# Two transformer layers in one kernel: weights of the second layer loaded into the first ffn's tiles, and a new order at the end of the second attention

## The chip, the cores and the metric

The kernel runs on one core of a Trainium2 chip. The metric is device time in microseconds (us) of one execution, the median of several runs. The engines are named as in the profile: PE is TensorE (PEld its weight loads), DVE is VectorE, ACT is ScalarE, POOL is GpSimd, and SP is SyncE, which here only issues DMAs. A name such as L921 is line 921 of the kernel before the change, unless the text says otherwise.

## The reference

The input is x of shape (4, 1024, 512): 4 sequences of 1024 tokens, 512 features, all in float32. Two layers follow each other, and each has the same outer form:

```
xn = layernorm(x)
x  = x + attention(xn) * silu(ffn(xn))
```

Layer 0's attention is linear attention with 16 heads of 32 features and an exponential decay per head, computed in chunks with a running state, between a qkv projection and an output projection. Its ffn is two linear layers with ternary weights, 512 to 2048 to 512, each behind a normalisation of its input, with gelu between them.

Layer 1's attention is softmax attention without a mask, 16 heads of 32 features. The first half of each head's q and k is rotated by position:

```
q, k, v = heads(x @ wq.T), heads(x @ wk.T), heads(x @ wv.T)
q, k    = rope on the first 16 of the 32 features of each head
y       = softmax(q @ k.T / sqrt(32)) @ v
return merge(y) @ wo.T
```

Layer 1's ffn has integer weights, from which 128 is subtracted, with a scale for each output feature:

```
lin(x, wq, scale) = x @ ((float(wq) - 128) * scale[:, None]).T
ffn(x) = lin(silu(lin(x, wq_gate, s_gate)) * lin(x, wq_up, s_up), wq_down, s_down)   # 512 -> 1408 -> 512
```

## The kernel before

The 4096 tokens are 32 tiles of 128 tokens (`NTILE`), in 8 blocks of 512 (`NBLK`, 4 tiles each, `TPB`). The kernel has four stages, one after the other: attention 0 (to about 628 us), the first ffn (to 1164), attention 1 (to 2668), and the second ffn (to the end). In the stages of interest the order of PE's instructions is the order in which the program writes them. The order on DVE, ACT, POOL and SP is made by a scheduler, except for operations that are marked with `tc.keep_in_program_order`, which keep their place among each other. Tiles come from pools with a fixed number of buffers, so that a new tile waits until its buffer's last reader is done.

**First ffn.** A loop over g takes one chunk c of 128 hidden features of one block per step (16 chunks, `NH0`). `hidden` (L563) makes the products `fc`, gelu on ACT, and the two halves hp (L583 on DVE) that carry a float32 value as two rounded parts; `proj` (L618) accumulates `pj`, some steps behind. `prep_in` (L541) loads a tile x0f of the next block and makes xq on DVE (L550) every third step. `gate` (L628) ends a tile: y (L640, DVE), tanh (ACT), two DVE products, the sum with x on POOL, the store of x1 on SP, and the moments of the new row for the next layernorm. `norm1` (L649) turns four rows' moments into scale and shift, with a root made of small DVE operations (`root`, L107). `wfc` are four tiles of 8 KB a partition.

**Start of attention 1.** Its pools open when those of the first ffn close. The weights wk, wq and wv are loaded by POOL DMAs (L752 to L758) into tiles of their own, wo later by SP. `heads_in` (L805) is a list of chains of products for one group of four heads: projections (L779), and the copies and the partial rotation of q and k, for which parts of raw tiles (tag `raw`, two buffers) are moved between partitions by DMAs (L830), with DVE L833 and POOL L835. `late` (L785) is the layernorm on ACT of the last four tiles, which the first ffn had not turned yet.

**Main loop of attention 1.** There are 32 units (sequence, group of four heads, half of the queries), and 8 steps a unit (`TB`), so 256 steps s; a second position e = s − 10 (`LAG`) runs behind. In step s PE does, in this order: two pairs of score products `sq` (`top`, L921), whose row maxima DVE reduces (`mx`, L925); the product y of e − 1 with v (`weigh`, L967); then the scores `sk` again, transposed, for e (`expo`: L948, and L954 which subtracts the maxima mT); and ACT makes the exponentials pT of e in two halves (L959, three buffers). At the end of a unit `turn_max` (L927) turns the maxima into mT (L937, DVE). POOL sums the eight pT of a unit into part (L1068, L1070); `total` (L858) and `divide` (L866) turn that sum into the divisor (zs, four reciprocals L874 on DVE) and yT (L875, POOL). For the last unit the sum is not made on POOL: PE totals each pT by itself (`z_last`). From s = 256 the loop has no `sq` any more, only the trailing y and sk. Products sq and sk share three buffers of two PSUM banks (`ring`). Between the pieces, `advance` lets PE do parts of chains that are queued: projections of the next group, or `wo_out` (L878), which makes four tiles of s and stores them (so, L892 and L893).

After the loop eight chains of `wo` remain, four of unit 30's half and four of the last.

**Second ffn.** `prep2` (L1090) loads xs and makes the two parts xp of a block (ACT copy L1097, DVE difference L1098). `weight` (L1105) loads a chunk of integer weights into `wint` (four buffers, L1111) and subtracts 128 on DVE (L1113); 33 chunks in the order of use. `gated` (L1134) makes gate and up (L1140), `down` (L1157) accumulates dn, `gate` (L1167) ends a tile: z, tanh (L1176), two products on DVE, the sum on POOL (L1179), the store (L1180). `most` (L1201) is the largest magnitude of each weight chunk; if one is above 4095, a second version of the whole ffn runs behind a branch, which these inputs never take.

Of the kernel before, what the change touches and what calls it, by code (L numbers as in the profile page):

```python
# [19 lines left out]
P = 128  # L20
# [15 lines left out]
def kernel(ctx, tc, ins, out):  # L36
# [44 lines left out]

    layer0 = ctx.enter_context(ExitStack())
# [42 lines left out]

    def transpose_to(dst, src, name, on_scalar):

        t = tr(f"tr_{name}")
        for k in range(4):
            nc.tensor.transpose(t[:, k, :], src[:, k * P : (k + 1) * P], ident)  # L130
        if on_scalar:
            nc.scalar.copy(dst, t)  # L132
        else:
            nc.vector.tensor_copy(dst, t)
# [8 lines left out]
    wfc = [f0w.tile([P, FF0], F32R, tag=f"wfc{k}", name=f"wfc{k}") for k in range(KD)]  # L143
# [383 lines left out]
    with ExitStack() as es:  # L527
# [8 lines left out]
        hparts, sums, mvs, x1s, xnTp = {}, {}, {}, {}, {}  # L536
# [4 lines left out]
        def prep_in(blk, i):  # L541
# [5 lines left out]
            x = p2.tile([P, D], F32, tag="x", name=f"x0f_{t}")  # L547
            nc.sync.dma_start(out=x, in_=x_t[t])
# [100 lines left out]
        def norm1(blk):  # L649

            ts = slice(blk * TPB, (blk + 1) * TPB)
            root(st1[:, ts, 1], 1e-5, p2, f"n{blk}", True)
            nc.vector.scalar_tensor_tensor(
                shift[:, ts], st1[:, ts, 0], -1.0, st1[:, ts, 1], ALU.mult, ALU.mult
            )

# [21 lines left out]
        pending = None  # L678
        for g in range(NH0 * NBLK + 2 + 2 * TPB):
            blk, c = divmod(g, NH0)  # L680
            if blk < NBLK:
                if c >= 2 and c % 3 == 2 and c < 2 + 3 * TPB and blk + 1 < NBLK:
                    pending = prep_in(blk + 1, (c - 2) // 3)
                hidden(blk, c)
                if blk == 0 and wpj0 + c < NH0:
                    ternary("pj", wpj0 + c, raw0("pj", wpj0 + c, "f"))
# [15 lines left out]
            if blk and (c == 12 or (blk == NBLK and c == 9)):  # L702
                norm1(blk - 1)
# [17 lines left out]
    s1_t = s1.rearrange("(t p) d -> t p d", p=P)  # L721
    with ExitStack() as es:
# [3 lines left out]

        w0 = es.enter_context(tc.tile_pool(name="a1w", bufs=1, reuse_waits="tile"))
# [12 lines left out]
        W, xnTs, heads = {}, {}, {}  # L740
# [11 lines left out]
        for n in ("wk", "wq", "wv", "wo"):  # L752
            W[n] = w0.tile([P, KD, D], F32, tag=n, name=n)
        for n in ("wk", "xnT", "wq", "wv"):
            if n == "xnT":
                load1(0)
                continue
            nc.gpsimd.dma_start(out=W[n], in_=ins[n + "T"].rearrange("(k p) n -> p k n", p=P))  # L758
        cs = w0.tile([P, 2, N], F32, tag="cs", name="cs")
# [25 lines left out]
        def late(i):  # L785
# [5 lines left out]
            nc.scalar.activation(  # L791
                xn, x, AF.Identity, bias=shift[:, t : t + 1], scale=st1[:, t, 1:2]
# [178 lines left out]

        es.enter_context(tc.manual_schedule(engines={mybir.EngineType.PE}))
# [4 lines left out]
        for c in heads_in(0, 0, spread):  # L977
            chain = c
            advance(8)
        must, spare = deque(), deque()  # L980
        mx, mTs, pTs, ys, parts, lates, soon = {}, {}, {}, {}, {}, {}, {}
        for s in range(TB * nu + LAG + 1):
# [25 lines left out]
            if s == 2 * TB:  # L1008
                tc.keep_in_program_order(
# [6 lines left out]
            if s < TB * nu:  # L1016
# [5 lines left out]
                if j == TB - 1:  # L1022
# [3 lines left out]
                    del mx[u]  # L1026
            if 1 <= e <= TB * nu:
# [4 lines left out]
                if u == nu - 1:  # L1032
# [3 lines left out]
                    total(z_last, pTs[e - 1], kb, TB)  # L1036
                pTs.pop(e - 2, None)
                if kb == TB - 1:
# [3 lines left out]
                    if u == nu - 1:  # L1042
                        divide(units[u], yr, z_last)
            held = 0
            if s % TB == 0 and 0 < s <= TB * nu:
                turn_max(s // TB - 1)
            elif s % TB == 4 and 0 <= s // TB - 2 < nu - 1:
                u = s // TB - 2
                z = ring(f"z_{u}")[:, 0, :] if s >= TB * nu else acc1(f"z_{u}")
                total(z, parts.pop(u), 0, 1)  # L1050
                divide(units[u], ys.pop(u), z)
                b, g, qh = units[u]
# [7 lines left out]
            if 0 <= e < TB * nu:  # L1060
                u, kb = divmod(e, TB)
                pT = pTs[e] = p2.tile([P, 4, 512], F32, tag="pT", name=f"pT_{e}", bufs=3)
                expo(u, kb, pT)
                if u == nu - 1:
                    pass
                elif kb == 1:
                    parts[u] = p2.tile([P, 4, 512], F32, tag="part", name=f"part_{u}")
                    nc.gpsimd.tensor_tensor(parts[u], pTs[e - 1], pT, ALU.add)  # L1068
                elif kb:
                    nc.gpsimd.tensor_tensor(parts[u], parts[u], pT, ALU.add)  # L1070
            advance(4 - held)
        for new in [*soon.values(), (*units[-1][::2], yTs[B - 1])]:
            spare.extend(wo_out(*new, spread))
        for chain in spare:
            advance(8)
# [5 lines left out]
    def ffn1_slots():  # L1081
# [8 lines left out]
        def prep2(blk):  # L1090

            b, h = divmod(blk, 2)
            xs = p2.tile([P, KD, BLK], F32, tag="xs", name=f"xs_{blk}", bufs=1)
            xp = [a.bitcast(F32R) for a in xpair(f"xp1_{blk}")]
            for k in range(KD):
                nc.sync.dma_start(out=xs[:, k, :], in_=xnT_d[b][k, :, h * BLK : (h + 1) * BLK])
                nc.scalar.copy(xp[0][:, k, :], xs[:, k, :])  # L1097
                nc.vector.tensor_tensor(  # L1098
                    xp[1][:, k, :], xs[:, k, :], xp[0][:, k, :].bitcast(F32), ALU.subtract
                )  # L1100
            return xp

        ws = {}

        def weight(n, c):  # L1105
            q = p2.tile([P, KD, P], I32, tag="wint", name=f"{n}_int{c}", bufs=4)
            if n == "down":
                src = ins["wq_downT"][c * P : (c + 1) * P, :].rearrange("p (k n) -> p k n", n=P)
            else:
                src = ins[f"wq_{n}T"][:, c * P : (c + 1) * P].rearrange("(k p) n -> p k n", p=P)  # L1110
            nc.sync.dma_start(out=q, in_=src)  # L1111
            w = ws[n, c] = wp.tile([P, KD, P], F32R, tag=f"{n}{c}", name=f"w{n}{c}")
            nc.vector.tensor_scalar(w, q, -128.0, None, ALU.add)  # L1113

        xp = prep2(0)
        sg = wp.tile([P, NH1], F32, tag="sg", name="sg")
        nc.sync.dma_start(out=sg, in_=ins["s_gate"])
        su = wp.tile([P, NH1], F32, tag="su", name="su")
        nc.sync.dma_start(out=su, in_=ins["s_up"])
        for c in range(NH1 + 2):  # L1120
            for n, d in (("gate", c), ("up", c), ("down", c - 2)):
                if 0 <= d < NH1:
                    weight(n, d)
        sdb = wp.tile([P, D], F32, tag="sdb", name="sdb")
        nc.sync.dma_start(out=sdb, in_=ins["s_down"].partition_broadcast(P))

        sg2 = wp.tile([P, NH1], F32, tag="sg2", name="sg2")
        nc.vector.tensor_scalar(sg2, sg, 0.5, None, ALU.mult)
        sgu = wp.tile([P, NH1], F32, tag="sgu", name="sgu")
        nc.vector.tensor_tensor(sgu, sg2, su, ALU.mult)  # L1130

# [190 lines left out]
    with ExitStack() as es1:  # L1322
        again = ffn1_slots()
# [77 lines left out]
```

## Time and profile before

| what | us |
|---|---|
| median of 3 runs | 3192.12 (3191.96 to 3195.52) |
| profiled execution | 3187.48 |
| its span in the profile | 3185.7 |
| PE busy in the span | 3103.5 |
| DVE busy | 1874.3 |
| POOL busy | 1512.6 |
| ACT busy | 1196.4 |
| last product of the first ffn ends | 1164.3 |
| last product of attention 1 ends | 2667.86 |
| first product of the second ffn starts | 2676.76 |
| last product of the second ffn ends | 3173.45 |

The times of instructions are those of the one profiled execution, counted from the start of its span. In a row of the waits, the columns are engine, line and operation that waited, what it waited for, the sum, the number of times and the longest. In a row of the timeline or of the chain, they are start, length, what ran, and in brackets the idle time before it and what ended that.

### The profile page before, as it was taken

To read this page: it belongs to the slowest core of one execution; us is meant where nothing else is said; L and a number is where in the kernel's file an instruction comes from. 1 tells how busy PE (TensorE), PEld (TensorE's weight loads), DVE (VectorE), ACT (ScalarE), POOL (GpSimd) and SP (SyncE) were. 2 spreads that over 40 slices of the span, in tenths; PEclk is the share of its full clock that TensorE was granted. 3 is DMA by queue.
4 is the path that set the end of the run, shared out by engine and by line. 5 is a ranking of instruction groups with operands and counts; after the bars stand their busy time and mean duration, and the time that the engine had idled before them with its cause. 6 is when DMAs were issued, how large, how long until landed. Compare 5 with 4: busy or idle time off the path is not lost.

```text
span 3185.7 us, 61092 instructions
## 1 busy us (share of the span) xinstructions
PE 3103.5 (97%) x26257; PEld 1763.6 (55%) x26257; DVE 1874.3 (59%) x2628; ACT 1196.4 (38%) x1695; POOL 1512.6 (47%) x618
## 2 busy tenths in 40 slices
PE   9999999999999989999999999999999988999998
PEld 5555555577777864344344444443344325888886
DVE  4444555478887866666555565655555634755554
ACT  2111111155655533444444444444444442333322
POOL 1000000034443445888988888988988850000001
PEclk9999999999999999999999999999999999999999
DMA  3111111212222331100001000100000005222112
GB/s 129 54 56 58 53 54 41 67 46 90 81 70 67 116 118 46 34 9 8 14 13 40 13 10 15 38 15 15 15 13 13 12 1 159 87 67 73 63 50 68
DMA packets 97655, 158.46 MB, mean 50 GB/s; under 512 B 13024, under 2 KB 26592, under 8 KB 97248
## 3 DMA queue, kind: packets, MB, share of 16 engines
q1 hardware_dynamic: 96560, 151.33, 15.2%
q8 instruction: 207, 3.39, 0.4%
q0 software_dynamic: 816, 3.15, 0.3%
q14 instruction: 72, 0.59, 0.1%
HBM read 104.10 MB, written 41.94 MB: 46 GB/s over the span
## 4 chain that ended last, share of the span: by engine, by line
PE 84%; DVE 10%; ACT 2%; issue 1%; DMA 1%; SPq 1%; POOL 1%; POOLq 0%; ACTq 0%; DVEq 0%
PE sk L948 9%; PE sq L921 8%; PE y L967 8%; PE qk L331 7%; PE dn L1162 5%; PE up L1140 5%; PE gate L1140 5%; PE v1ps L779 4%; PE wq L779 3%; PE v0ps L305 3%; PE wo L314 3%; PE wo L779 3%; PE pj L623 3%; PE wk L779 3%; PE fc L570 3%; PE sk L954 2%
## 5 line engine op out<-in xcount | busy, mean ns | idle before, releaser
L1070 POOL TENSOR_TENSOR part<-part,pT 128x2048 f32<-128x2048 f32 x186 | 854.4, 4594 | 19.3 <-ACT pT L959 10.0
L925 DVE TENSOR_REDUCE mx<-sq 128x2 f32<-128x1024 f32 x512 | 603.7, 1218 | 398.6 <-PE sq L921 397.5
L959 ACT ACTIVATE pT<-sk 128x1024 f32<-128x1024 f32 x512 | 496.4, 1022 | 625.5 <-PE sk L954 619.6
L948 PE MATMUL sk<-wqT,wkT 32*128 32x512 f32 x2048 | 325.8, 640 | 3.7 <-DVE mx L925 3.7
L921 PE MATMUL sq<-wkT,wqT 32*128 32x512 f32 x2048 | 320.3, 638 | 8.3 <-ACT pT L959 6.3
L967 PE MATMUL y<-pT,v 128*32 128x512 f32 x2048 | 283.5, 606 | 12.8 <-ACT pT L959 12.8
L1179 POOL TENSOR_TENSOR th<-th,x 128x512 f32<-128x512 f32 x32 | 41.4, 1293 | 493.6 <-DVE th L1178 393.0
L623 PE MATMUL pj<-wpj,hp 128*128 128x512 f32 x1024 | 265.8, 397 | 8.3 <-DVE hp L583 7.2
L591 POOL TENSOR_TENSOR sums<-sums,h 128x512 f32<-128x512 f32 x112 | 164.0, 1465 | 229.7 <-ACT h L575 220.9
L570 PE MATMUL fc<-xp,wfc 128*128 128x512 f32 x1024 | 261.5, 398 | 3.0 <-ACT h L575 2.1
L954 PE MATMUL sk<-mT,onesr 2*128 2x512 f32 x1024 | 236.2, 785 | 0.0
L338 POOL TENSOR_TENSOR qd<-qT,wqkv 128x512 f32<-128x512 f32 x32 | 43.1, 1346 | 404.7 <-ACT qT L336 379.2
L331 PE MATMUL qk<-xnT,wqkv 128*128 128x512 f32 x512 | 228.3, 599 | 0.7 <-ACT xnT L132 0.7
L623 PEld LDWEIGHTS pj<-wpj,hp 128*128 128x128 f32 x1024 | 190.1, 188 | 60.9 <-DVE hp L583 20.2
L570 PEld LDWEIGHTS fc<-xp,wfc 128*128 128x128 f32 x1024 | 187.9, 189 | 44.3 <-ACT h L575 5.0
L1140 PE MATMUL gate<-xp,wgate 128*128 128x512 f32 x704 | 180.1, 398 | 8.9 <-DVE wgate L1113 8.9
L1140 PE MATMUL up<-xp,wup 128*128 128x512 f32 x704 | 179.5, 396 | 1.0 <-DVE h L1147 1.0
L1162 PE MATMUL dn<-wdown,hp 128*128 128x512 f32 x704 | 177.8, 394 | 0.0
L1068 POOL TENSOR_TENSOR part<-pT,pT 128x2048 f32<-128x2048 f32 x31 | 141.1, 4553 | 71.2 <-ACT pT L959 71.2
L948 PEld LDWEIGHTS sk<-wqT,wkT 32*128 32x128 f32 x2048 | 97.4, 183 | 134.6 <-issue 113.8
L583 DVE TENSOR_TENSOR hp<-h,hp 128x512 fp32r<-128x512 f32 x128 | 119.1, 931 | 78.0 <-ACT hp L580 77.7
L967 PEld LDWEIGHTS y<-pT,v 128*32 128x32 f32 x2048 | 41.8, 108 | 214.4 <-issue 186.2
(216 smaller groups left out, 4566.9 us busy)
## 6 DMA issues: line engine op xcount, KB each, us to landing
s<-s SPq DMA_DIRECT2D x96, 256.0 KB
x<-x SPq DMA_DIRECT2D x36, 256.0 KB
x<-in_x SPq DMA_DIRECT2D x32, 256.0 KB
raw_fc<-in_w_fcT SPq DMA_DIRECT2D x32, 256.0 KB
x0f<-in_x SPq DMA_DIRECT2D x32, 256.0 KB
x0r<-in_x SPq DMA_DIRECT2D x32, 256.0 KB
x<-th SPq DMA_DIRECT2D x32, 256.0 KB
xnT<-xnT_d SPq DMA_DIRECT2D x8, 1024.0 KB
```

The costliest lines, as they stand in the source:

```text
L331: nc.tensor.matmul(a, lhsT=wqkv[k][:, c0 : c0 + P], rhs=xnTs[blk][:, k, :], start=(k == 0), stop=(k == KD - 1),)
L570: nc.tensor.matmul(a, lhsT=wfc[k][:, c * P : (c + 1) * P], rhs=xp[n][:, k, :].bitcast(F32R), start=(k == 0 and n == 0), stop=(k == KD - 1 ...
L623: nc.tensor.matmul(ds[i], lhsT=hparts[blk, c][n][:, i * P : (i + 1) * P], rhs=wpj[c], start=(c == 0 and n == 0), stop=(c == NH0 - 1 and n ...
L779: nc.tensor.matmul(out[r0 : r0 + HD, :], lhsT=lhsT[:, r0 : r0 + HD], rhs=rhs, start=start, stop=stop,)
L921: nc.tensor.matmul(sq[:, hh, :], lhsT=qT[r, q0 : q0 + P], rhs=kT[r, n * 512 : (n + 1) * 512], start=True, stop=True,)
L925: nc.vector.tensor_reduce(mx[:, qt, 2 * pair : 2 * pair + 2, n], sq, AX.X, ALU.max)
L948: nc.tensor.matmul(sks[h // 2][:, h % 2, :], lhsT=kT[r, kb * P : (kb + 1) * P], rhs=qT[r, qh * 512 : (qh + 1) * 512], start=True, stop=False,)
L959: nc.scalar.activation(pT[:, 2 * pair : 2 * pair + 2, :], sks[pair], AF.Exp, scale=QKS)
L967: nc.tensor.matmul(y[r, :], lhsT=v[:, kb, r], rhs=pT[:, h, :], start=(kb == 0), stop=(kb == TB - 1),)
L1070: nc.gpsimd.tensor_tensor(parts[u], parts[u], pT, ALU.add)
L1140: nc.tensor.matmul(a, lhsT=ws[n, c][:, k, :], rhs=xp[m][:, k, :], start=(k == 0 and m == 0), stop=(k == KD - 1 and m == 1),)
L1162: nc.tensor.matmul(ds[i], lhsT=hparts[blk, c][n][:, i * P : (i + 1) * P], rhs=w, start=(c == 0 and n == 0), stop=(c == NH1 - 1 and n == 1),)
```

## The change

Six parts, told in the order of the kernel.

1. A pool `w0` with four tiles of [128, 4, 512] float32 is opened before layer 0 and stays to the end. `wfc` of the first ffn uses these tiles; then wk, wq, wv and wo of attention 1; then the first 16 weight chunks of the second ffn, four to a tile. The POOL DMAs for wk, wq and wv are issued at the first step of the first ffn's closing phase, in a row.
2. In the first ffn the loads x0f are issued two steps before `prep_in` uses them.
3. `norm1` of the last block moves from the end of the first ffn into attention 1, behind the fourth chain of the first `heads_in`; the ACT operation of `late` keeps its program order.
4. The scales sg and su and their products become constants outside the second ffn.
5. End of attention 1: in each of the steps 244 to 255 one weight chunk of the second ffn is loaded into a raw tile and one converted (two in the last). From step 256 on, the scores sk and exponentials of e come before y of e − 1. The sums of pT move from POOL to DVE for those steps; the last unit's second four pT are summed there too, and its one total and its `divide` stand behind the second of the remaining `wo` chains. Unit 30's total comes two steps later. The parts xp of the second ffn's first block are made before the last four `wo` chains.
6. Second ffn: the other 21 weight chunks and the xs parts go through one tag `stage` of six buffers; s, x, z and th have four buffers; the very last tile is finished in two halves, with its sum on DVE; the `most` reductions keep their program order.

The core of the diff:

```diff
+    es1 = ExitStack()
+    w0 = es1.enter_context(tc.tile_pool(name="w0", bufs=1, reuse_waits="tile"))
+    shared = ("wk", "wq", "wv", "wo")
+    def shared_tile(tag, name):
+        return w0.tile([P, KD, D], F32, tag=tag, name=name)
...
-    wfc = [f0w.tile([P, FF0], F32R, tag=f"wfc{k}", name=f"wfc{k}") for k in range(KD)]
+    wfc = [
+        shared_tile(tag, f"wfc{k}").rearrange("p k n -> p (k n)").bitcast(F32R)
+        for k, tag in enumerate(shared)
+    ]
...
+        W = {}
         for g in range(NH0 * NBLK + 2 + 2 * TPB):
             blk, c = divmod(g, NH0)
+            if g == NH0 * NBLK:
+                for n in ("wk", "wq", "wv"):
+                    W[n] = shared_tile(n, n)
+                    tc.keep_in_program_order(
+                        nc.gpsimd.dma_start(
+                            out=W[n], in_=ins[n + "T"].rearrange("(k p) n -> p k n", p=P)
+                        )
+                    )
             if blk < NBLK:
...
+                if c % 3 == 0 and c < 3 * TPB and blk + 1 < NBLK:
+                    t = (blk + 1) * TPB + c // 3
+                    x0fs[t] = p2.tile([P, D], F32, tag="x", name=f"x0f_{t}")
+                    nc.sync.dma_start(out=x0fs[t], in_=x_t[t])
...
-            if blk and (c == 12 or (blk == NBLK and c == 9)):
-                norm1(blk - 1)
+            if blk and c == 12:
+                norm1(blk - 1, p2)
...
+    def weight(stage, pool, pinned=False):
+        m = len(ws)
+        n, c = needed[m]
+        q = stage(f"{n}_int{c}").bitcast(I32).rearrange("p (k n) -> p k n", n=P)
+        if n == "down":
+            src = ins["wq_downT"][c * P : (c + 1) * P, :].rearrange("p (k n) -> p k n", n=P)
+        else:
+            src = ins[f"wq_{n}T"][:, c * P : (c + 1) * P].rearrange("(k p) n -> p k n", p=P)
+        load = nc.sync.dma_start(out=q, in_=src)
+        j = m // 4
+        if j not in fours:
+            tag = quads[j] if j < len(quads) else f"wf{j}"
+            fours[j] = pool.tile([P, KD, D], F32, tag=tag, name=f"wf{j}")
+        w = ws[n, c] = fours[j][:, m % 4, :].bitcast(F32R).rearrange("p (k n) -> p k n", n=P)
+        if pinned:
+            tc.keep_in_program_order(load)
+        def less():
+            op = nc.vector.tensor_scalar(w, q, -128.0, None, ALU.add)
+            if pinned:
+                tc.keep_in_program_order(op)
+        return less
...
+    def parts1(blk, stage, pinned=False):
+        b, h = divmod(blk, 2)
+        xp = [a.bitcast(F32R) for a in xpair(f"xp1_{blk}")]
+        for k in range(KD):
+            xs = stage(f"xs_{blk}_{k}")
+            each = [
+                nc.sync.dma_start(out=xs, in_=xnT_d[b][k, :, h * BLK : (h + 1) * BLK]),
+                nc.scalar.copy(xp[0][:, k, :], xs),
+                nc.vector.tensor_tensor(
+                    xp[1][:, k, :], xs, xp[0][:, k, :].bitcast(F32), ALU.subtract
+                ),
+            ]
+            if pinned:
+                for op in each:
+                    tc.keep_in_program_order(op)
+        return xp
...
-        for c in heads_in(0, 0, spread):
+        for m, c in enumerate(heads_in(0, 0, spread)):
             chain = c
             advance(8)
+            if m == 3:
+                norm1(NBLK - 1, p2)
...
+        def exps(e):
+            if not 0 <= e < TB * nu:
+                return
+            u, kb = divmod(e, TB)
+            pT = pTs[e] = p2.tile([P, 4, 512], F32, tag="pT", name=f"pT_{e}", bufs=3)
+            expo(u, kb, pT)
+            k0 = TB // 2 if u == nu - 1 else 0
+            add = nc.vector if e + LAG >= TB * nu else nc.gpsimd
+            if kb == k0 + 1:
+                parts[u] = p2.tile([P, 4, 512], F32, tag="part", name=f"part_{u}")
+                add.tensor_tensor(parts[u], pTs[e - 1], pT, ALU.add)
+            elif kb > k0:
+                add.tensor_tensor(parts[u], parts[u], pT, ALU.add)
...
+            late_exp = s >= TB * nu
+            if late_exp:
+                exps(e)
...
+                    if kb < TB // 2:
+                        total(z_last, pTs[e - 1], kb, TB)
...
+            zu = (s - (6 if s >= TB * nu else 4)) // TB - 2
...
+            if TB * nu - 12 <= s < TB * nu:
+                nxt = weight(raw1, w0, True)
+                if loaded:
+                    loaded()
+                loaded = nxt
+                if s == TB * nu - 1:
+                    loaded()
+        soon = [*soon.values()]
+        for new in soon:
+            spare.extend(wo_out(*new, lambda name: ring(name)[:, 0, :]))
+        for m, chain in enumerate(spare):
+            advance(8)
+            if m == 1:
+                total(z_last, parts.pop(nu - 1), TB - 1, TB)
+                divide(units[-1], ys.pop(nu - 1), z_last)
+        xp1 = parts1(0, raw1, True)
+        for chain in wo_out(*units[-1][::2], yTs[B - 1], spread):
...
+        def stage(name):
+            return p2.tile([P, 512], F32, tag="stage", name=name, bufs=6)
+        xp = xp1
+        while len(ws) < len(needed):
+            weight(stage, w0 if len(ws) < 4 * len(quads) else wp)()
...
+            last = t == NTILE - 1
+            for h in range(2 if last else 1):
+                c = slice(h * D // 2, (h + 1) * D // 2) if last else slice(0, D)
+                nc.vector.tensor_tensor(z[:, c], d[:, c], sdb[:, c], ALU.mult)
+                nc.scalar.activation(th[:, c], z[:, c], AF.Tanh, scale=0.5)
+                nc.vector.scalar_tensor_tensor(th[:, c], th[:, c], 1.0, z[:, c], ALU.add, ALU.mult)
+                nc.vector.scalar_tensor_tensor(th[:, c], th[:, c], 0.5, s[:, c], ALU.mult, ALU.mult)
+                (nc.vector if last else nc.gpsimd).tensor_tensor(th[:, c], th[:, c], x[:, c], ALU.add)
+                nc.sync.dma_start(out=out_t[t][:, c], in_=th[:, c])
```

## The prediction

> **What bounds the kernel now.** I read the page's shares first. PE is busy for 97% of the span and holds most of the chain that ended last, so time can only come from the 3% in which PE stands, from PE running behind a slower clock, and from the ends of the span.
>
> ```profile
> PE 3103.5 (97%) x26257; PEld 1763.6 (55%) x26257; DVE 1874.3 (59%) x2628; ACT 1196.4 (38%) x1695; POOL 1512.6 (47%) x618
> PE 84%; DVE 10%; ACT 2%; issue 1%; DMA 1%; SPq 1%; POOL 1%; POOLq 0%; ACTq 0%; DVEq 0%
> ```
>
> A table of 80 us windows then finds that 3%. The columns behind the window are its length, busy time (instructions) of PE, PEld, DVE, ACT and POOL, the granted clock, the DMA share and GB/s.
>
> ```profile
> 1120.00:1200.00 80.00, 69.56 (x755) 52.22 (x753) 51.27 (x105) 30.24 (x50) 33.23 (x25) 0.98 0.34 110
> 2480.00:2560.00 80.00, 77.36 (x822) 29.71 (x816) 51.69 (x45) 33.82 (x40) 68.44 (x18) 0.98 0.03 10
> 2560.00:2640.00 80.00, 65.83 (x444) 18.24 (x440) 22.76 (x21) 34.49 (x38) 35.09 (x10) 1.00 0.00 1
> 2640.00:2720.00 80.00, 70.08 (x678) 50.28 (x671) 45.27 (x87) 20.86 (x35) 1.28 (x1) 0.94 0.61 191
> 2720.00:2800.00 80.00, 80.00 (x345) 64.42 (x344) 53.20 (x83) 25.75 (x41) 5.17 (x4) 1.00 0.19 60
> ```
>
> PE misses 10 to 14 us in each of three windows, and 2720 to 3120 has none to give: the second ffn runs at PE's own pace. The waits of PE name the holes, first from 2580 to 2720, then from 1160 to 1200:
>
> ```profile
> PE y L967 <- ACT pT L959: 12.8, 11, 1.2
> PE gate L1140 <- DVE wgate L1113: 8.9, 1, 8.9
> ```
> ```profile
> PE v1ps L779 <- DVE wqT L833: 3.1, 1, 3.1
> PE wq L779 <- DMA wq<-in_wqT: 2.5, 1, 2.5
> PE wq L779 <- DVE wkT L833: 1.7, 1, 1.7
> PE sq L921 <- POOL wqT L835: 1.5, 1, 1.5
> ```
>
> The 12.8 is not all that the tail loses. The chain in order of time shows the last steps as one file of links: scores, exponential, y, total, next scores.
>
> ```profile
> 2608.47 1.07 PE sk L948 x8
> 2609.86 1.03 ACT pT L959
> 2610.94 1.54 PE y L967 x6
> 2612.91 0.86 PE z_last L861 x6
> 2613.76 1.07 PE sk L948 x8
> ```
>
> From 2608.4 to 2634.9 a step takes 5.30, five times in a row. PE's work in it is sk 1.07, its max part 0.28, y 1.00 and total 0.86, which is 3.21; the rest is PE waiting for ACT.
>
> **The change, part by part** (us; minus is gained; against the profiled execution of 3187.48).
>
> *Start of the first ffn.* The waits of PE there are 0.9 for s L319 and 4.3 in four for hp L583. Issuing x0f two steps early takes its load out of the xq products' way and moves two of them, and one wpj, off DVE's queue ahead of hp_0_4; the longest wait is 2.65. DVE's products L550 take 0.50 alone and up to 1.52 when POOL is adding. I take two of 0.6 = −1.2; ends −2.5 (the whole 2.65) and 0 (another DVE step is late next).
>
> *First ffn to attention 1.* The three weight DMAs leave POOL ahead of the adds th_28 to th_31 (before, wq was issued at 1167.44, behind an add from 1165.78), so the 2.5 for wq goes, and norm1's chain (1176.56 to 1179.0) leaves DVE, so the 1.7 goes. But the path to the first sq does not run there. It is SP: x<-th L646 waits for POOL's th_31 (ends 1175.6), x_28's load is at 1176.11, and behind it 32 loads of raw_wk and raw_wq parts at 0.7 each end at 1198.67, feeding wqT at 1197.27 and sq at 1197.32. In the new DVE order the moments of row 29 stand before y_31 and wait for POOL, so y_31 ends about 1170.3 (1168.87 before), th_31 about 1176.55, and SP's file shifts by +1.0. I take +1.0: PE gets the same file of waits, redistributed. Ends: −1.5 (the waits of wq and wkT, 4.1, less what the file gives back) and +3.0 (norm1's 2.4 on DVE now ahead of late's first activation).
>
> *sg, su and their products at the kernel's start* cost nothing: two 0.4 issues on SP near 20 us, 0.33 on DVE near 30, between v products with PE's weights still loading; uncovered they would cost 0.7.
>
> *Steps 244 to 255, the twelve early conversions.* Each step gains a 256 KB load on SP (0.5; the window to 2560 moves 10 GB/s) and one conversion on DVE, 0.42 in its row:
>
> ```profile
> L1113 DVE TENSOR_SCALAR wgate<-gate_int x11: 416/423/429, 2676.2 to 2708.2; 128x512 fp32r<-128x512 int32 x11
> ```
>
> These ran with POOL idle; now POOL adds 128x2048 tiles, 4.53 each with 0.08 between. Behind each conversion on DVE are the two reductions mx (1.22 each) that free sq's banks. The nearest rows: neg_pj L189, a TENSOR_SCALAR from SBUF to SBUF, 0.48 alone, took 1.51 and ended 0.29 after POOL's instruction; mT L937 has 0.74 at least and 5.01 at most:
>
> ```profile
> 2589.47 3.72 DVE L937 SCALAR_TENSOR_TENSOR mT<-mh,second,mf 128x512 fp32r<-128x512 f32 x1 [5.74 <-ACT mh L935]
> 2574.32 27.86 POOL L1070 TENSOR_TENSOR part<-part,pT 128x2048 f32<-128x2048 f32 x6
> ```
>
> The fourth of those six adds ends at 2592.64, mT at 2593.19. The reductions L925 take 1.22 beside POOL too. So I let a conversion end 0.29 after the running add, and the next add start that much later. DVE's step is then 2.44 + 0.29 with the rest spent waiting, inside POOL's 4.9, and PE's step (2.26 + 1.00 + 1.35 = 4.61) keeps up by its spare banks. Followed step by step this makes the adds 1.1 late by the last one, and attention's end 1.4 later. Bounds: 0 (no blocking) and 12 × (4.53 + 0.29) = 57.8 (each conversion waits a whole add and PE with it).
>
> [...]
>
> *Tail of attention 1.* sk of step e now precedes y of e−1, so a step costs PE its own 3.21 and no wait for ACT (two exps, 1.94). The start is set on DVE: add 246 has moved there from POOL and stands before mT(31). It waits for POOL's add 245, 2592.64 + 1.1 = 2593.75, takes 2.28 (the 128x2048 add L467), and mT 0.55: 2596.6. Step 249's sk then starts at 2598.0 (2602.25 before). From there three steps of 3.21, one of 3.21 + 0.86 with unit 30's z, two of 2.35 without a total, then exp 255, which also waits for add 253 on DVE (exp 253 ends 2615, + 2.28 = 2617.3, no wait), and the last y's: wo starts at 2621.0 against 2639.65, −18.65. z_last's one late total stands among the wo chains, +0.86. Sum −17.8, conversions included; wo, 28.2, ends at 2649.8 against 2667.86. Cover that could fail: yT for the fifth chain is ready at 2621 + 0.86 + 7.0 (two chains) + 0.59 (zs) + 3.39 (four reciprocals) + 1.26 = 2634.1, needed 2636, 1.9 to spare. Ends −21.5 (no conversion blocks) and −8 (mT or an add late for every step).
>
> *Seam.* Before, the first gate product waited 8.90 for weights that SP issued at 2671.79, behind so's stores and four xs loads. Now twelve weights are there, and xp needs xs, whose loads sit on SP behind the stores so_3 and so_4 (2637 onward), land about 3.7 later as before (2668.99 to 2672.73), then copies and differences: ready about 2646, needed 2650. −8.9; the end on the other side is 0.
>
> *Cold start and weight rate behind it.*
>
> ```profile
> 2676.76 3.75 PE L1140 MATMUL gate<-xp,wgate 128*128 128x512 f32 x8 [8.90 <-DVE wgate L1113]
> 2716.54 1.86 PE gate L1140 x8
> ```
>
> Eight gate products took 3.75 after the idle stretch, 1.86 later, with the clock at 0.94 in this window. At that pace u3, behind seven groups (7 × 1.87 + 0.46), would have started at 2690.3; it started at 2693.5. −3.2. The 21 other weights come through six buffers; 33 took 40 before, 1.2 each, and weight 13 is needed 18.7 after the start: no stall. [...]
>
> *End.* The last tanh waits for a store, since th has two buffers:
>
> ```profile
> 3177.31 0.63 ACT L1176 ACTIVATE th<-z 128x512 f32<-128x512 f32 x1 [2.68 <-DMA out<-th]
> ```
>
> With four it starts near 3174.2; the row in two halves with its add on DVE, beside POOL's th_30, ends at 3178.75, where POOL ended at 3180.78. −2.0, ends −1.0 and −3.2. The max reductions `most` go from DVE's idle time at 2676 to 2739 into 33 later steps, 0.69 each, where DVE is two thirds busy: nothing.
>
> Sum: −1.2 + 1.0 − 17.8 − 8.9 − 3.2 − 2.0 = −32.1. 3187.48 − 32.1 = 3155.4 for a profiled execution. The median of the runs shown, 3192.12, lies 4.6 above the profiled one; I carry that on: 3160.0. All lower ends together give −40.3.
>
> **The rivals.** 0.2%, about 6.4 us, is what a measurement here can tell from no change.
>
> 1. *Conversions eat half of it.* Each waits half an add, 2.27 + 0.29 = 2.6, and half of that reaches PE through the banks that mx frees: 12 × 1.3 = 16, so −16, 3176. For: POOL is busy 68 of 80 in that window, and a banked reduction behind a blocked conversion frees nothing. Against: DVE is busy 52 of 80, PE has three bank pairs.
> 2. *The seam keeps its wait,* for xp instead of weights (SP's stores, or ACT's copies behind so, late): −8.9 and −3.2 fall away, −20, 3172. For: 4 us of margin worked out through four queues. Against: the loads are issued 13 us before they are needed.
> 3. *Slower.* One mechanism: in steps 244 to 255 a conversion waits for a whole add, the reductions behind it hold PE, and POOL's next add waits for the exponential that PE delays, so nothing overlaps. It decides from 32.1 / 12 = 2.7 a step; at the full 4.82 it is 57.8 − 32.1 + 1.4 (counted above) = +27, 3219.
> 4. *The change does not do what it says:* the last steps stay in file because ACT takes exp e only after PE's y has freed a pT buffer (three). Then the tail gives −4 (mT's earlier start), the sum −18, 3174. Against: pT of e−3 is free two steps before.
>
> **How the numbers follow.** Forecast case (−26 to −40) 0.60; rival 1 0.14, rival 2 and 4 0.12 together; nothing measurable, between rivals 1 and 3, 0.05; slower 0.09. Faster is 0.60 + 0.14 + 0.12 = 0.86. The forecast's own range is 3152 to 3166. Eight in ten must take in rivals 1, 2 and 4 with some more blocking: 3152 to 3184.
>
> **What would show it.** Right: wo starts near 2621 in the new trace, no wait of PE over 1 at the seam, its window at clock 1.00, steps 2.4 to 3.2 apart from 250, L1176's last wait gone, the first sq about 1 later than 1197.3 (counted from the end of the first ffn). Wrong: conversions of 3 to 5 with PE waiting for mx in steps 244 to 255; a first gate product waiting for L1098's successor; wo's fifth chain waiting for yT.

## The result

The changed kernel took 3148.71 us (median of 4 runs, 3146.93 to 3150.13) beside 3193.82 for the kernel before: a ratio of 0.9855, 95% interval 0.9838 to 0.9873. A second set of four later gave 3154.84 beside 3191.16, 0.9884 (0.9866 to 0.9902). So it is faster, by 36 to 45 us, where 32 was forecast; the first set lies below the forecast range. The profiled executions, 3187.48 and 3149.29, differ by 38.2. By stage of the two traces, with the prediction's terms beside:

| stage | before | after | change | predicted |
|---|---|---|---|---|
| start to first fc | 628.8 | 630.5 | +1.7 | 0 |
| first ffn, to its last pj | 535.6 | 533.7 | −1.9 | −1.2 |
| last pj to first sq | 32.95 | 33.99 | +1.0 | +1.0 |
| first sq to last wo | 1470.5 | 1459.7 | −10.8 | −17.8 |
| last wo to first gate | 8.90 | −0.07 | −9.0 | −8.9 |
| second ffn, first gate to last dn | 496.7 | 479.2 | −17.5 | −3.2 |
| last dn to the end | 12.25 | 10.53 | −1.7 | −2.0 |
| sum | | | −38.2 | −32.1 |

Five terms came as worked out or within 2 us. Two did not: the tail of attention gave 7 less, and the second ffn 14 more. The windows of the changed kernel, in the columns shown before:

```profile
2480.00:2560.00 80.00, 77.81 (x800) 29.59 (x792) 55.29 (x48) 32.00 (x39) 62.09 (x18) 0.91 0.10 29
2560.00:2640.00 80.00, 76.14 (x640) 27.80 (x634) 54.50 (x39) 38.63 (x44) 34.54 (x9) 0.96 0.09 27
2640.00:2720.00 80.00, 80.00 (x599) 62.53 (x593) 43.66 (x75) 27.78 (x45) 1.27 (x1) 1.00 0.55 178
2720.00:2800.00 80.00, 80.00 (x354) 66.24 (x354) 47.49 (x71) 24.32 (x39) 7.78 (x6) 1.00 0.23 73
```

PE waits for 4 us where it waited 14 (second row), and for nothing behind 2640. But the granted clock is 0.91 and 0.96 in the tail, where it was 0.98 and 1.00. And the last row holds 354 products where the kernel before had 345 in the same 80 us, PE busy throughout in both, the clock at 1.00 in both. The waits of PE from 2480 to the end show what is late next:

```profile
PE sk L1033 <- DVE mT L1016: 2.2, 1, 2.2
PE sk L1027 <- DVE mx L1004: 1.8, 3, 0.7
PE sq L1000 <- ACT pT L1038: 1.3, 4, 0.3
```

The waits for pT at y (12.8) and for the first weights (8.9) are gone; mT takes their place, for 2.2. From 1155 to 1220 the waits only changed hands:

```profile
PE v1ps L856 <- DVE wqT L912: 5.8, 1, 5.8
PE wk L856 <- DVE y L658: 2.3, 1, 2.3
...
PE sq L1000 <- POOL wqT L914: 0.4, 1, 0.4
```

Wk's second half now waits 2.3 for y_31 (1.0 before), since the moments of row 29 stand ahead of it on DVE, and v1ps 5.8 where it was 3.1; y_31 ended at 1169.99 and the last th sum at 1176.22, near the 1170.3 and 1176.55 forecast.

### The profile page after: what moved, and what is told of

The parts are those of the page before. It is cut to its first block, busy times and chain, and to the rows that moved or that the text cites. A ratio compares the mean times of both kernels' runs of the same rounds, so it can differ in the third digit from the quotient of the medians.

```text
span 3147.5 us, 61092 instructions
## 1 busy us (share of the span) xinstructions
PE 3088.4 (98%) x26233; PEld 1765.4 (56%) x26233; DVE 1905.1 (61%) x2638; ACT 1196.1 (38%) x1696; POOL 1501.4 (48%) x615
## 4 chain that ended last, share of the span: by engine, by line
PE 84%; DVE 11%; issue 2%; ACT 2%; POOL 1%; SPq 1%; DMA 0%; ACTq 0%; POOLq 0%; DVEq 0%
PE sk L1027 9%; PE sq L1000 8%; PE y L1046 8%; PE qk L350 7%; PE gate L1218 5%; PE up L1218 5%; PE dn L1240 5%; PE v1ps L856 4%; PE v0ps L324 3%; PE wo L333 3%; PE wo L856 3%; PE wq L856 3%; PE fc L588 3%; PE wk L856 3%; PE pj L641 3%; PE sk L1033 2%
## 5 line engine op out<-in xcount | busy, mean ns | idle before, releaser
L1067 POOL TENSOR_TENSOR part<-part,pT 128x2048 f32<-128x2048 f32 x184 | 844.8, 4591 | 25.7 <-ACT pT L1038 16.5
L1027 PE MATMUL sk<-wqT,wkT 32*128 32x512 f32 x2048 | 332.5, 645 | 4.3 <-DVE mx L1004 4.3
L1046 PE MATMUL y<-pT,v 128*32 128x512 f32 x2048 | 276.3, 610 | 0.2 <-ACT pT L1038 0.2
L1218 PE MATMUL gate<-xp,wf 128*128 128x512 f32 x704 | 174.1, 389 | 0.0
L1218 PE MATMUL up<-xp,wf 128*128 128x512 f32 x704 | 173.8, 389 | 0.0
L1240 PE MATMUL dn<-wf,hp 128*128 128x512 f32 x704 | 173.5, 389 | 0.0
L350 PEld LDWEIGHTS qk<-xnT,wqkv 128*128 128x128 f32 x512 | 95.2, 191 | 112.8 <-issue 104.2
```

What stands on the lines that cost most here:

```text
L350: nc.tensor.matmul(a, lhsT=wqkv[k][:, c0 : c0 + P], rhs=xnTs[blk][:, k, :], start=(k == 0), stop=(k == KD - 1),)
L1027: nc.tensor.matmul(sks[h // 2][:, h % 2, :], lhsT=kT[r, kb * P : (kb + 1) * P], rhs=qT[r, qh * 512 : (qh + 1) * 512], start=True, stop=False,)
L1046: nc.tensor.matmul(y[r, :], lhsT=v[:, kb, r], rhs=pT[:, h, :], start=(kb == 0), stop=(kb == TB - 1),)
L1067: add.tensor_tensor(parts[u], parts[u], pT, ALU.add)
L1218: nc.tensor.matmul(a, lhsT=ws[n, c][:, k, :], rhs=xp[m][:, k, :], start=(k == 0 and m == 0), stop=(k == KD - 1 and m == 1),)
L1240: nc.tensor.matmul(ds[i], lhsT=hparts[blk, c][n][:, i * P : (i + 1) * P], rhs=w, start=(c == 0 and n == 0), stop=(c == NH1 - 1 and n == 1),)
```

## Experiments

**Comparing at one clock.** Executions of one kernel scatter by 10 us and more, and their times go with the mean granted clock of each. Over 37 executions of the kernel before, the clock goes from 0.997 (3183.8 us) to 0.991 (3200.1); a line through them is 3176.1 us plus 2.88 for each 0.001 of missing clock, and single runs lie 2.2 around it. "At equal clock" below is the mean of a kernel's runs, each moved along this slope to 0.995. (0.001 of 3190 us is 3.2 us, so a slope near that is what lost PE time alone would give.) There the kernel before stands at 3190.5, the changed one at 3145.0 and 3148.4 in its two sets (3146.7): −44. These two sets of one kernel lie 3.4 apart, so a difference of that size between the edits below is not told from nothing.

### The pace of the second ffn

My theory 1 came from the built programs' layouts: in the kernel before, the second ffn's weights start 224 bytes past a multiple of 256, while xp and hp start at 96; in the changed one all three start at 96. Part 4 takes four 64-byte tiles out of the weight pool, two of them ahead of the weights, and so shifts the weights by 128. In the changed kernel that holds for 17 of the 33 chunks; the other 16 stand in w0, which part 1 opens right behind xp. The traces show no addresses; what the runs test is the shifts. Theory 2: the pace came from the loads or from other engines' work. Four edits of the kernel before:

```diff
e1_scales: sg, su, sg2, sgu from the pool f1w to const, their loads and products behind s1_t (part 4 alone)
e1_pad256, e1_pad_w: at the start of pool f1w, with 64 or 32 elements
+        pad0 = wp.tile([P, 64], F32, tag="pad0", name="pad0")
+        nc.vector.memset(pad0, 0.0)
e1_pad_hp: the same with 32 elements, behind the weights and ahead of sdb
```

> The kernel before with part 4 of the change alone: sg, su and their two products become constants, and four 64-byte tiles leave the second ffn's weight pool. Each weight tile then starts 96 bytes past a multiple of 256, as xp and hp do, where it stood at 224. Theory 1 (SBUF placement sets the pace of the second ffn's products): the pace falls from 234 to 227 ns a product, 2112 products, so -14 us against the kernel before, and the waits at the seam and in attention's tail stay as they were. Theory 2 (the pace came from something else in the change, such as the weights' loads or the other engines' work): 234 ns stays, 0 us.

> The kernel before with an unused tile of 256 bytes a partition ahead of the second ffn's weights: everything behind it moves by 256, nothing by a part of that. Theory 1 with a period of 256: 234 ns a product, 0 us. If any new layout changes the pace, or if the pace is drawn anew for each program: something else than 234. It is also a second profile of what is nearly the kernel before.

> The kernel before with an unused tile of 128 bytes ahead of the second ffn's weights: weights at 96 past a multiple of 256, hp behind them at 224. gate and up have the moving operand xp at 96 and the stationary weights at 96; dn has moving weights at 96 and stationary hp at 224. Theory 1a (the difference between stationary and moving operand counts): gate and up at 227, dn at 234, -9.5 us. Theory 1b (an operand at 224 is slow only as weights, or as moving operand of dn): all at 227, -14 us. Theory 2: 0 us.

> The kernel before with an unused tile of 128 bytes behind the second ffn's weights and ahead of hp: weights stay at 224, hp moves from 96 to 224. gate and up as before (96 and 224), dn has both operands at 224. Theory 1a (the difference counts): dn at 227, gate and up at 234, -4.7 us. Theory 1b (an operand at 224 is slow by itself): all at 234 or slower, 0 us or more. Theory 2: 0 us.

The window from 2740 to 3060 lies inside the second ffn in every kernel. Here is its row in each of them.

Kernel before:

```profile
2740.00:3060.00 320.00, 320.00 (x1375) 257.56 (x1374) 174.71 (x258) 98.53 (x156) 27.23 (x21) 1.00 0.21 67
```

e1_pad256, all shifted by 256:

```profile
2740.00:3060.00 320.00, 320.00 (x1375) 257.57 (x1374) 179.16 (x268) 100.58 (x159) 25.91 (x20) 1.00 0.22 66
```

e1_pad_hp, hp shifted by 128:

```profile
2740.00:3060.00 320.00, 320.00 (x1385) 259.48 (x1384) 181.15 (x270) 101.27 (x160) 25.88 (x20) 1.00 0.21 66
```

e1_pad_w, weights and hp shifted by 128:

```profile
2740.00:3060.00 320.00, 320.00 (x1400) 262.82 (x1399) 178.76 (x265) 101.02 (x159) 27.69 (x22) 1.00 0.22 67
```

e1_scales, part 4 alone:

```profile
2740.00:3060.00 320.00, 320.00 (x1414) 264.87 (x1413) 182.99 (x271) 101.77 (x161) 28.44 (x22) 1.00 0.23 70
```

Changed kernel:

```profile
2740.00:3060.00 320.00, 320.00 (x1414) 264.86 (x1413) 199.34 (x300) 101.60 (x160) 28.48 (x22) 1.00 0.21 66
```

PE is busy for all of it at full clock; only the number of products differs. 320 us / 1375 is 232.7 ns a product, 320 / 1414 is 226.3. Part 4 alone brings the whole step: 2112 products by 6.4 ns are 13.5 us, and e1_scales stands at 3177.0 at equal clock, −13.5 (median 3176.47, ratio 0.9968, 0.9945 to 0.9991). A shift by 256 changes nothing (3189.5, −1.0). The two shifts by 128 divide it, as theory 1a says: −8.6 with weights and xp alike (3181.9), −4.1 with weights and hp alike (3186.4). The groups of PE in the same window, of e1_pad_w and then of e1_pad_hp (busy us and mean ns of one behind the bar), name the products:

```profile
L1164 PE MATMUL dn<-wdown,hp 128*128 128x512 f32 x464 | 117.4, 395 | 0.0
L1142 PE MATMUL up<-xp,wup 128*128 128x512 f32 x469 | 116.3, 390 | 0.0
L1142 PE MATMUL gate<-xp,wgate 128*128 128x512 f32 x466 | 115.3, 389 | 0.0
```
```profile
L1142 PE MATMUL up<-xp,wup 128*128 128x512 f32 x464 | 117.7, 395 | 0.0
L1142 PE MATMUL gate<-xp,wgate 128*128 128x512 f32 x457 | 115.7, 394 | 0.0
L1164 PE MATMUL dn<-wdown,hp 128*128 128x512 f32 x463 | 115.2, 391 | 0.0
```

With weights at 96 and hp at 224, dn is the slow one; with both at 224, dn is the fast one. So it is not a place that is slow, but a difference of 128 between the stationary and the moving operand. Theory 2 falls: in the three padded kernels nothing of the loads or of DVE's work had changed but one memset.

The same from the other side, an edit of the changed kernel, and one in its first ffn:

```diff
a_w0_pad: ahead of the shared tiles
+    pad0 = w0.tile([P, 32], F32, tag="pad0", name="pad0")
+    nc.vector.memset(pad0, 0.0)
a_f0_pad: ahead of the later wpj tiles of the first ffn
+        pad1 = p2.tile([P, 16], F32, tag="pad1", name="pad1", bufs=1)
+        nc.vector.memset(pad1, 0.0)
```

> The changed kernel with an unused tile of 128 bytes ahead of the four shared tiles: wfc, the second ffn's weights and hp all move to 224 past a multiple of 256, xp stays at 96. Theory 1a (difference of stationary and moving operand): gate and up (96 and 224) go from 227 to 234 ns, 1408 products, +9.4 us; dn (224 and 224) stays at 227; fc of the first ffn (96 and 224) goes from 230 to 234, +4 us or somewhat more; sum +13 us. Theory 2 (the pace comes from elsewhere in the change): 0 us.

> The changed kernel with an unused tile of 64 bytes ahead of the first ffn's working tiles: the hp parts of the first ffn and the later six wpj tiles move from 32 to 96 past a multiple of 256, where the other ten wpj stand, so that all operands of pj stand at 96. Theory 1a, if it holds for a difference of 64 as for 128: pj goes from 230.8 to 227 ns, 1024 products, -4 us. If only a difference of 128 counts: 0 us.

a_w0_pad gives the pace back: its second ffn takes 489.0 us against 479.2 (+9.8), and at equal clock the kernel stands at 3157.8, +11. fc went from a median of 230 to 232 ns, but the first ffn's blocks only from 66.60 to 66.7: there other waits fill in. a_f0_pad shows that more plainly. pj's median fell from 231 to 227 as forecast for a difference of 64, yet a block fell only from 66.60 to 66.4, and the kernel to 3145.2 at equal clock (median 3148.83), −1.5 instead of −4, which is within what two sets of one kernel differ by. One thing stays open: six of the sixteen wpj stood at 32 like hp, a difference of nothing, and ran at 231 as well; the difference is not the whole rule.

### The tail of attention 1

Theory 3: the conversions wait for POOL's adds, stretch the steps and hold mT. DVE's timeline of the changed kernel shows the waiting:

```profile
2591.77 2.18 DVE L783 TENSOR_SCALAR wf<-gate_int 128x512 fp32r<-128x512 int32 x1
2593.87 4.78 DVE L783 TENSOR_SCALAR wf<-up_int 128x512 fp32r<-128x512 int32 x1
2598.57 2.28 DVE L1067 TENSOR_TENSOR part<-part,pT 128x2048 f32<-128x2048 f32 x1
2600.78 0.74 DVE L1016 SCALAR_TENSOR_TENSOR mT<-mh,second,mf 128x512 fp32r<-128x512 f32 x1
```

The int32 conversion, 0.42 alone, took 4.78 and ended 0.28 after POOL's add (2598.37). Nine of the twelve early conversions took 2.2 to 4.8, and each of them ended 0.28 to 0.30 after one of POOL's adds of 4.5 to 4.6; the other three began with no add running on POOL and took 0.36 to 0.42. So in these steps a conversion that met an add ended just behind it, as the prediction let it (0.29). Two edits take the conversions out of DVE's file in those steps:

```diff
a_conv_tail:
-            if TB * nu - 12 <= s < TB * nu:
+            if TB * nu - 1 <= s < TB * nu + LAG + 1:
...
-                if s == TB * nu - 1:
+                if s == TB * nu + LAG:
a_conv_act, for the twelve early ones:
-            op = nc.vector.tensor_scalar(w, q, -128.0, None, ALU.add)
+                op = nc.scalar.activation(w, q, AF.Identity, bias=m128)
```

> The changed kernel with the twelve early weight loads and conversions moved from steps 244 to 255 into steps 255 to 266, where POOL adds nothing any more. Theory 3 (DVE's conversions wait for POOL's adds, hold the reductions behind them and so PE, and the last one holds mT): no conversion over 0.45 us, step 255's sq 6 us earlier, mT of the last unit 5 us earlier, wo's start 5 to 10 us earlier, time -5 to -10 us against the changed kernel. Rival 3b (the tail lost its time to a slower clock, whatever DVE did): conversions short, but wo's start within 2 us of the changed kernel's. Rival 3c (the conversions are now late for the seam): PE waits over 1 us at the second ffn's first products.

> The changed kernel with the twelve early conversions on ACT instead of DVE, in the same steps 244 to 255 (later ones stay on DVE). Theory 3: ACT does not wait for POOL, a conversion takes some 0.6 us (as a copy of this size does), the steps 248 to 255 return to 4.5 to 6.1 us each and mT comes 5 us earlier: -5 to -8 us. Rival 3d (the conversions cost by being in any engine's file in these steps, or the loads cost): no gain, within 2 us. A new tile of 64 bytes moves all operands by 64 together, so by theory 1a the pace stays at 227 ns.

The profiles look as theory 3 said: in a_conv_tail no conversion over 0.43 and mT 5.2 us earlier behind the first sq; in the two, first sq to last wo 1454.1 and 1455.6 against 1459.7. But ahead of mT the changed kernel's profile has 13.7 us at half clock and a_conv_tail's 3.4, and half of that difference is 5.1. The times do not follow: medians 3152.42 and 3147.36, at equal clock 3148.4 and 3146.6 against 3146.7. The difference between the profiles is the clock. The table of windows, first of the changed kernel, then of a_f0_pad, which has the same conversions in the same steps, then of e1_pad256, which has none:

```profile
2540.00:2556.00 16.00, 15.93 (x68) 5.12 (x66) 10.42 (x10) 5.08 (x6) 11.60 (x3) 0.57 0.15 42
...
2604.00:2610.00 6.00, 6.00 (x31) 1.59 (x28) 0.00 (x0) 2.52 (x4) 0.00 (x0) 0.50 0.02 3
```
```profile
2544.00:2560.00 16.00, 15.45 (x96) 5.49 (x96) 15.37 (x13) 8.27 (x10) 15.10 (x4) 1.00 0.18 50
```
```profile
2556.00:2580.00 24.00, 23.93 (x100) 7.02 (x102) 9.11 (x8) 6.99 (x8) 12.21 (x3) 0.57 0.00 1
```

In the changed kernel's profile PE ran 13.7 us at half clock from 2541.8 and 6.8 more from 2603.2; in a_f0_pad the first stretch is missing, and ten steps (sk of e = 235 to 245) take 52.2 us instead of 57.8. e1_pad256, nearly the kernel before, ran 20.5 us at half clock in the same part. Half of such a stretch is, by estimate, lost time where PE is busy throughout (the eight products y of a step took 1.94 twice in the one from 2541.8, and 1.07 behind it): 10.2 us in the changed kernel's attention 1, 1.7 in the profile of the kernel before. Without them the term is −10.8 − 8.5 = −19.3, where −17.8 was forecast. Taken off in the same way, first sq to last wo is an estimated 1449.5 in the changed kernel (1451.2 in after_again below), 1450.7 in a_conv_tail and 1448.8 in a_conv_act: the rival that the clock made the difference (3b) fits, a gain of 5 us or more does not. So theory 3 holds for what DVE does and falls for what it costs: the conversions lengthen the ten steps by some 2.5 us (52.2 against 51.4 in the kernel before, with 1.7 of half clock in that), where I had 1.1, and at equal clock hardly any of it is left; it seems to go into the wait for POOL's last add, which mT needs with or without them.

Then the order of exponentials and the early weights:

```diff
a_file:
-            late_exp = s >= TB * nu
+            late_exp = False
a_no_early: without the block "if TB * nu - 12 <= s < TB * nu:" that loads and converts twelve chunks
```

> The changed kernel with one line undone: from step 256 the scores and exponentials of e stay behind y of e - 1, as in the kernel before. Forecast's account of the tail (the steps wait for ACT): steps of 5.3 us return where 3.2 and 2.3 stood, seven of them, so wo starts some 16 us later. Rival 4 of the prediction (pT's buffers hold the exponentials anyway): within 2 us of the changed kernel.

> The changed kernel without the twelve early weights: all 33 are loaded and converted in the second ffn, through its six buffers. Forecast's account: PE stands some 6 to 9 us between wo and the first gate product and runs some 2 to 4 us behind a slow clock and late weights, while the steps 244 to 255 return to their old length (6 us) and mT is 5 us earlier: in all 0 to +3 us against the changed kernel, that is, the early weights as placed earn about nothing. If the conversions cost less than theory 3 says: +10 us or more.

a_file took 3169.08 (3162.72 to 3177.99; 3166.1 at equal clock, +19), first sq to last wo 1472.0, and this row of PE's waits is back:

```profile
PE y L1046 <- ACT pT L1038: 12.4, 11, 1.2
```

The order alone is the tail's gain; the prediction's rival 4 falls. a_no_early took 3158.48 (3151.6 at equal clock: +5, or +3.2 against the changed kernel's set beside it), with the wait at the seam back at 4.9 instead of 8.9:

```profile
PE gate L1210 <- DVE wf L783: 4.9, 1, 4.9
```

The second ffn behind it took 480.6, +1.4. So the early weights earn 6.4 us there (4.98 and 1.4) and cost some 1.5 to 3 before, by what is left at equal clock. Of the −8.9 for the seam, 4.0 need no early weights; that this is because the loads no longer stand behind xs on SP is argued, not shown.

### A version past both, and the changed kernel again

b_best puts together the late conversions, a_f0_pad's tile, and mT ahead of add 246:

```diff
-                add.tensor_tensor(parts[u], parts[u], pT, ALU.add)
+                def plus():
+                    return add.tensor_tensor(parts[u], parts[u], pT, ALU.add)
+                if e + LAG == TB * nu:
+                    return plus
+                plus()
...
                 turn_max(s // TB - 1)
+                if late_exp:
+                    tc.keep_in_program_order(plus())
...
and mT of the last unit keeps its program order
```

> The changed kernel with the conversions in steps 255 to 266, mT of the last unit ahead of DVE's add 246, and the 64-byte tile that puts pj's operands at 96. Theory 3: mT waits for POOL's add 245 alone and ends 3 us earlier than with the conversions moved alone (2597.7 against a first sq at 1199.5), wo's end 1453 to 1451 us behind the first sq; -6 to -10 us against the changed kernel. Rival 3e (something else, such as ACT's exponentials or the granted clock, is late right behind mT): no more than the moved conversions alone give, -5.

> The changed kernel once more, beside the others on one chip, with a second profile. The first profile lay 38 us under that of the kernel before, the medians 45. If a half-speed clock in some stretches of attention 1 makes the difference (theory 4), executions of both kernels scatter by some 10 us, and this profile's stages differ from the first changed one's only where the granted clock does; the second ffn's blocks take 59.84 us in both.

DVE's timeline of b_best:

```profile
2591.53 3.27 DVE L1018 SCALAR_TENSOR_TENSOR mT<-mh,second,mf 128x512 fp32r<-128x512 f32 x1 [6.23 <-ACT mh L1016]
2594.73 2.28 DVE L1072 TENSOR_TENSOR part<-part,pT 128x2048 f32<-128x2048 f32 x1
```

mT ends at 2594.80, 1.4 us earlier behind the first sq than in a_conv_tail, not 3. But this profile has 6.8 us at half clock ahead of it where a_conv_tail's has 3.4, an estimated 1.7 more lost. b_best took 3145.93 (3139.86 to 3154.59; 3143.0 at equal clock) beside 3154.84 for the changed kernel on the same chip, ratios to the kernel before 0.9866 (0.9841 to 0.9891) and 0.9884 (0.9866 to 0.9902): perhaps 4 us better, which these runs do not show, as the intervals overlap. after_again is as theory 4 says: its second ffn took 479.16 us again, its seam −0.07, its runs went from 3149.11 at clock 0.995 to 3158.05 at 0.992.

## Why the prediction was wrong, and where it was right

**The failed step** is the pace of the second ffn, which the sum left as it was: "the second ffn runs at PE's own pace", and "sg, su and their products at the kernel's start cost nothing". I priced their instructions, rightly (the first fc starts at 629.0 in e1_scales, at 628.8 before), and not what leaves with them: 128 bytes ahead of the weights. Nor did I ask where w0 puts the other weights; no run parts the two in the changed kernel. The term that took the difference is the second ffn, −3.2 forecast, −17.5 measured: −13.5 is the pace by placement (−12.8 between the second ffns of these two profiles, 496.7 and 483.9). The rest, −4.0 to −4.8, stands where the cold start was forecast: the kernel before runs at half clock from 2671.7 to 2681.9, 5.1 us of it behind the first product, and the changed one has no such stretch there. With the −13.5 the sum would have been −45.6; at equal clock the kernels are 44 apart. I read 1.86 for eight gate products as PE's own pace because PE was busy for 80.00 of 80; busy at a slower pace looks the same in that column.

**The tail** was mis-sized in the profile, −10.8 for −17.8, by half-clock stretches of 8.5 us that no step of the sum had, not by the step's own mechanism. wo started at 2628.8 where 2621.0 was forecast, but the steps behind the last half-clock stretch came as worked out, 3.16, 4.02, 2.30 and 2.52 for 3.21, 4.07, 2.35 and 2.35:

```profile
2612.79 1.14 PE L1027 MATMUL sk<-wqT,wkT 32*128 32x512 f32 x8
2615.95 1.14 PE L1027 MATMUL sk<-wqT,wkT 32*128 32x512 f32 x8
2619.97 1.14 PE L1027 MATMUL sk<-wqT,wkT 32*128 32x512 f32 x8
2622.27 1.13 PE L1027 MATMUL sk<-wqT,wkT 32*128 32x512 f32 x6
2624.79 1.13 PE L1027 MATMUL sk<-wqT,wkT 32*128 32x512 f32 x6
```

Within the tail, the two conversions of step 255 stood ahead of add 246, which I had left out: mT came at 2601.5 instead of 2596.6, which cost less than it looks: an estimated 6.8 us had been lost to the clock ahead of it.

**From profile to median** I carried 4.6 us on. The scatter by clock is larger: the kernel before's profile, 3187.48, was among its faster executions.

**The first ffn's start** came as −1.9 for −1.2, but most of it is a half-clock stretch of 3.4 us at 651, which that profile of the kernel before has: with one, the first ffn takes 535.6 before and 534.9 with the change (a_conv_act), without one 534.0 (e1_pad256) and 533.7. The earlier loads earn 0.3 to 0.7. The +1.7 ahead of it is such a stretch at 12.5.

**As forecast:** first ffn to attention +1.0 (SP's file; of the two waits that were to go, wq's load went and wkT fell from 1.7 to 1.2); the seam −9.0; the end −1.7, with the last tanh no longer waiting for a store:

```profile
3136.93 1.31 ACT L1259 ACTIVATE th<-z 128x512 f32<-128x512 f32 x3 [2.13 <-DVE z L1258]
```

Rival 1 named the right wait, of conversions for POOL's adds, at 16 us, where the ten steps grew by some 2.5; rivals 2 and 3 did not occur. Two small sums of the prediction are off, without bearing on the forecast: its lower ends add up to −40.8, not −40.3, and wo would by its own terms end at 2650.1, not 2649.8.

## What to carry to other kernels

A tile that is added or dropped moves every tile behind it: compare the layouts of the two builds, not only their instructions, and count products in a fixed window where PE is busy throughout. Where runs scatter, plot time against the mean granted clock before reading a difference of some us; two profiles can differ by more than the edit does. And pair what waits in a tail by issuing the next step's input ahead of this step's use, which was the largest gain meant here.

## What the runs showed of the chip

- In the second ffn the time of a 128x128 by 128x512 fp32r product depends on where its operands start: 226.3 ns from start to start with stationary and moving operand alike modulo 256 bytes, 232.7 with 128 between them, in gate and up alternating between 229 and some 237. A shift by 256 has no effect (x1375 in both). Why 128 bytes matter is open, and the six wpj of the first ffn do not fit.
- The stretches at half clock that end inside the span last 3.4, 6.8, 10.2, 13.7 or 20.5 us in these traces, multiples of 3.4. At the seam they go with idle time: in the five profiles where PE stands for 8.9 to 9.3 us ahead of the second ffn, 10.2 us at half clock begin 2.5 to 4.2 us into the wait (3.8 in the kernel before); a_no_early, with 4.9, has 3.4; the changed kernel, with none, has none. In attention 1 idle time ahead of them does not show: the longest idle stretch of PE in the 10 us ahead of the 13.7 us at 2541.8 was 0.72, and a_f0_pad had the same 0.73 there and kept its clock. What starts those stretches is open.
